# Attention values of two neighbouring groups computed in one go in the fused turns

## The chip, the cores and the metric

The kernel runs on one core of a Trainium2 chip. Its engines work side by side and meet at semaphores: TensorE (PE, with its weight loads listed apart as PEld), VectorE (DVE), ScalarE (ACT), GpSimd (POOL) and SyncE (SP), which issues DMAs. The metric is the device time of one launch in microseconds (us). The kernel before took 914.95 us (median of three runs, 913.76 to 915.36).

## The reference

One decoder layer on 16 sequences of 256 tokens with 256 channels, all in float32. Three blocks follow each other, and after each the sum with its input is normalised over the channels:

```
x = _layernorm(x + attn(x))       # 4 heads against 1024/4 fixed keys and values, relu(scores)**2, no softmax
x = _layernorm(x + xattn(x, ctx)) # 16 heads of 16 channels, softmax, below
x = _layernorm(x + ffn(x))        # 256 -> 1024 -> 256, with a low-rank addition chosen by the largest gate of 8
```

The middle block is the one that the change touches:

```
logits = jnp.einsum('bhqd,bhkd->bhqk', Q, K) * scale
D = jnp.clip(frac[:, None, :] - frac[:, :, None], CLAMP_MIN, CLAMP_MAX)
D_pos = jnp.maximum(D, 0.0)
D_neg = jnp.minimum(D, 0.0)
stoich_bias = ap * D_pos[:, None] + an * D_neg[:, None]
attn = gamma * logits + delta * stoich_bias
probs = jax.nn.softmax(attn, axis=-1)
out = jnp.einsum('bhqk,bhkd->bhqd', probs, V)
```

## The kernel before, in words

The order of the instructions on every engine is written out by hand; each engine works through its own list, and semaphores are set where one engine needs another's data or buffer.

The kernel has three stretches. In the first (to about 260 us) the eight blocks of 512 tokens go through the first attention. Then 64 groups follow, one per turn of the loop at line 1014 (index n): a group is four heads of one sequence, all 256 queries against all 256 keys. A sequence has four groups (og = n % 4): two chunks o of eight heads, and in each chunk the even heads (i = 0) and the odd heads (i = 1). A last stretch after the loop ends the feed-forward work of the last two blocks.

The stages of one group are spread over three turns. In its own turn n, PE computes the logits (L609) into four PSUM banks, on top of a bias that ACT has put there before ("positive", L600: the preload, one per bank g), DVE adds the other bias and finds the row maxima (L624), and POOL and DVE subtract them (L639). In turn n+1 PE transposes the result (L649, g = 0 to 3) and ACT takes the exponential on the way out of PSUM (L656, into `pT`). In turn n+2 `attend` (L665) multiplies it with the values and a column of ones: a *value set* of eight matmuls of a 32-column array shape, which the profile lists as 16 records, since every float32 matmul is listed twice. The set of the even heads fills one half of an accumulator bank `av`, that of the odd heads the other; after the odd one `keep` copies the bank out (L678, DVE).

From n = 15 (FIRST) to n = 62 the turns are *fused*: beside a group each turn carries an eighth of a block's feed-forward work. `tb` counts the blocks (0 to 5) and `part` (0 to 7) the eighth. Part 0 turns the block's rows (L749, copied by ACT, L752), part 1 computes the gates, parts 2 and 3 ("halved") the first large products, and parts 4 to 7 one product each with the second weights (`finish`: L860 on PE, 16 records, then L873 and statistics on DVE).

In a turn of parts 4 to 7 PE's list is: logits of group n; the value set of group n-2; transposes g = 0 and 1 of group n-1; a *large piece* (one of queries L437, project L561, keys L457, values L479, by n % 4); the product L860; transposes g = 2 and 3. ACT's list is: the exps g = 2 and 3 of the turn before, a fourth bias (L593), the preloads g = 0 and 1, exp 0, preload 2, exp 1, preload 3, and then what the part adds, in part 7 four scalings of the next block's rows (L249).

Small PSUM results go to three tiles that are handed out in rotation (`tile_b`): two of the pool psB and one of psV. A new tile may be written when the engine that read the third last one is done. The accumulator `av` has a bank of its own, `pT` two buffers.

Of the kernel before, what the change touches and what calls it, by code (L numbers as in the profile page):

```python
# [21 lines left out]
def tile_decoder_layer(ctx: ExitStack, tc: tile.TileContext, a: dict, out: bass.AP):  # L22
# [364 lines left out]
    if True:  # L387
# [296 lines left out]
        groups = [Group(batches[n // 4], n % 4) for n in range(4 * B)]  # L684
        N = len(groups)
# [209 lines left out]
    with tc.manual_schedule():  # L895
# [20 lines left out]
        for tb in range(NB):  # L916
# [24 lines left out]
            if tb > 1:  # L941
                older = rows_in[tb - 2]
# [67 lines left out]
        FUSED, FIRST = NB - 2, 15  # L1010
# [3 lines left out]
        for n in range(N + 2):  # L1014
            now, nxt, last, older = (
                groups[n + d] if 0 <= n + d < N else None for d in (0, 1, -1, -2)
            )
            large_piece, small_piece, more = pieces(n)
            tb, part = divmod(n - FIRST, 8)
            ff = rows_out[tb] if 0 <= tb < FUSED or (tb == FUSED and part < 2) else None  # L1020
            halved = ff and part in (2, 3)
# [2 lines left out]
            done = None  # L1024
            if part == 3 and 0 < tb < FUSED or (tb, part) == (FUSED, 0):
                done = rows_out[tb - 1]
            b, og = divmod(n, 4)

            if n < 2:
# [4 lines left out]
                six.gates()  # L1034
            if n > N:
                six.inner(0, range(0, 1))
            if older and not halved and n != N:
                older.attend()
            if nxt:
                nxt.negative(4 if 1 <= n < FIRST - 1 else 3)  # L1040
# [103 lines left out]
            tb, part = divmod(n - FIRST + 4, 8)  # L1144
# [116 lines left out]
```

## Time and profile before

| | |
|---|---|
| median of the runs | 914.95 us (913.76 to 915.36) |
| the profiled execution's own time | 914.93 us |
| its span | 913.1 us |
| PE busy | 892.4 us (98%) |
| DVE busy | 707.7 us (78%) |
| ACT busy | 584.2 us (64%) |
| POOL busy | 379.5 us (42%) |
| granted TensorE clock | 1.00 |
| value sets, L665 | 1024 records, 69.8 us |
| logits, L609 | 1024 records, 74.8 us |

A busy share says how long an engine had something in hand; matmuls are pipelined, so the extents of neighbouring rows overlap, and the start of one group of rows to the start of the next is the better measure of what it takes. The length of a turn is taken from its first logits to the first logits of the next turn. For the block from n = 23 to n = 30 the lengths are 7.41, 7.32, 15.34, 14.06, 9.59, 9.16, 9.16 and 9.24 us (parts 0 to 7); for the three blocks after it part 0 takes 7.14 us and parts 4 to 7 the same as here. In the last fused block, whose turns have fewer large pieces, parts 4 to 7 take 9.16, 7.43, 9.15 and 7.43 us.

### The profile page before, as it was taken

The numbers are of one execution on the slowest core, as the hardware profiler recorded it, in microseconds if no ns is written. First come the engines' busy times: TensorE is split into PE (matmuls) and PEld (weight loads), VectorE is DVE, ScalarE is ACT, GpSimd is POOL, SyncE is SP. The second block draws the span as 40 slices with busy tenths as digits, with TensorE's granted clock in tenths as the row PEclk, the third lists the DMA queues.
The fourth block names the chain that finished last, engine by engine and source line by source line (L and its number), as shares of the span: only waits on it lengthen the run. The fifth ranks groups of instructions, "written<-read, shape, count | busy, mean of one in ns | idle before, by whom it ended". The sixth has DMA issues, their size and how long they took to land.

```text
span 913.1 us, 19025 instructions
## 1 busy us (share of the span) xinstructions
PE 892.4 (98%) x6910; PEld 541.6 (59%) x6910; DVE 707.7 (78%) x1968; ACT 584.2 (64%) x977; POOL 379.5 (42%) x369
## 2 busy tenths in 40 slices
PE   6999999999999999999999999999999999999997
PEld 2333333333356776577658757865875686586555
DVE  5788899889878998778777877777787787678443
ACT  4757877787687879466666856665685567556111
POOL 1002312231469996434635543463454336244010
PEclk9999999999999999999999999999999999999999
DMA  5411011100001222010111202011120201111001
GB/s 137 146 36 35 30 36 41 65 1 2 3 11 50 70 71 56 13 42 21 35 43 39 52 13 66 18 37 41 40 52 14 65 17 40 41 27 45 23 1 47
DMA packets 44190, 37.01 MB, mean 41 GB/s; under 512 B 14912, under 2 KB 40000, under 8 KB 44096
## 3 DMA queue, kind: packets, MB, share of 16 engines
q1 hardware_dynamic: 43536, 35.52, 14.0%
q8 instruction: 55, 0.90, 0.4%
q14 instruction: 39, 0.32, 0.1%
q10 hardware_dynamic: 560, 0.26, 0.1%
HBM read 21.07 MB, written 6.03 MB: 30 GB/s over the span
## 4 chain that ended last, share of the span: by engine, by line
PE 56%; ACT 4%; DVE 1%; issue 1%; ACTq 0%; DVEq 0%
PE ps_b L860 12%; PE ps_l L830 12%; PE ps_b L649 9%; PE ps_l L609 6%; PE ps_v L665 5%; PE ps_b L561 3%; PE ps_b L457 2%; PE ps_b L479 2%; PE ps_l L842 2%; ACT ps_l L600 2%; ACT pT L656 1%; PE ps_b L437 1%; PE ps_b L749 1%; ACT qT L447 1%; DVE neg L624 1%
## 5 line engine op out<-in xcount | busy, mean ns | idle before, releaser
L588 POOL TENSOR_SCALAR neg<-dneg,aneg,delta 128x512 f32<-128x512 f32 x205 | 175.7, 869 | 211.2 <-ACT pT L656 185.8
L624 DVE CUSTOM_DVE_ANT_0 neg<-ps_l,neg 128x256 f32<-128x256 f32 x512 | 181.6, 420 | 43.0 <-PE ps_l L609 39.8
L600 ACT ACTIVATE ps_l<-dpos,apos_d 128x512 f32<-128x512 f32 x256 | 173.1, 686 | 34.5 <-DVE mx L624 30.5
L656 ACT ACTIVATE pT<-ps_b 128x512 f32<-128x512 f32 x256 | 143.3, 590 | 59.1 <-PE ps_b L649 57.4
L324 DVE TENSOR_TENSOR pr<-r 128x1024 f32<-128x1024 f32 x128 | 155.5, 1255 | 32.4 <-ACT r L322 32.1
L322 ACT ACTIVATE r<-ps_a 128x1024 f32<-128x1024 f32 x128 | 126.5, 1022 | 59.1 <-PE ps_a L314 33.9
L649 PE MATMUL ps_b<-ident,neg 128*128 128x128 f32 x1024 | 140.3, 278 | 4.0 <-ACT pT L656 2.4
L649 PEld LDWEIGHTS ps_b<-ident,neg 128*128 128x128 f32 x1024 | 112.9, 140 | 41.9 <-issue 15.3
L639 POOL TENSOR_TENSOR neg<-neg,mx 128x1024 f32<-128x1024 f32 x65 | 124.3, 1914 | 30.0 <-DVE mx L624 24.0
L314 PE MATMUL ps_a<-xnT,kT 64*64 64x512 f32 x1024 | 124.2, 601 | 0.0
L334 PE MATMUL ps_v<-pr,vv 64*64 64x512 f32 x1024 | 123.5, 593 | 0.3
L860 PE MATMUL ps_b<-wof,hT 128*128 128x256 f32 x512 | 115.8, 380 | 0.0
L830 PE MATMUL ps_l<-xt,wi 128*128 128x512 f32 x256 | 115.0, 596 | 0.8 <-ACT hT L849 0.8
L860 PEld LDWEIGHTS ps_b<-wof,hT 128*128 128x128 f32 x512 | 96.4, 190 | 16.0 <-issue 2.3
L639 DVE TENSOR_TENSOR neg<-neg,mx 128x1024 f32<-128x1024 f32 x63 | 90.9, 1443 | 0.3
L349 POOL TENSOR_TENSOR xt<-xt,half 128x512 f32<-128x512 f32 x15 | 23.7, 1583 | 141.0 <-ACT half L348 141.0
L334 PEld LDWEIGHTS ps_v<-pr,vv 64*64 64x64 f32 x1024 | 38.1, 132 | 70.7 <-issue 43.7
L314 PEld LDWEIGHTS ps_a<-xnT,kT 64*64 64x64 f32 x1024 | 38.1, 135 | 67.9 <-issue 56.2
L830 PEld LDWEIGHTS ps_l<-xt,wi 128*128 128x128 f32 x256 | 46.8, 190 | 52.0 <-issue 45.8
L609 PE MATMUL ps_l<-kM,qT 32*128 32x256 f32 x1024 | 74.8, 401 | 0.4 <-ACT ps_l L600 0.4
L665 PE MATMUL ps_v<-pT,vaug 128*32 128x256 f32 x1024 | 69.8, 385 | 0.8 <-ACT pT L656 0.8
L853 DVE TENSOR_SCALAR hT<-ps_l,wib 128x512 f32<-128x512 f32 x44 | 30.5, 745 | 42.8 <-PE ps_l L842 42.8
(107 smaller groups left out, 966.9 us busy)
## 6 DMA issues: line engine op xcount, KB each, us to landing
cT<-in_ctxT SPq DMA_DIRECT2D x16, 256.0 KB
kM<-keys SPq DMA_DIRECT2D x128, 32.0 KB
v<-raw SPq DMA_DIRECT2D x128, 32.0 KB
invs<-rows SPq DMA_DIRECT2D x128, 32.0 KB
x<-in_x SPq DMA_DIRECT2D x7, 512.0 KB
out<-x SPq DMA_DIRECT2D x7, 512.0 KB
frow<-in_frac SPq DMA_DIRECT2D x16, 128.0 KB
wi<-in_wiT SPq DMA_DIRECT2D x1, 1024.0 KB
```

What stands on the lines that cost most here:

```text
L314: nc.tensor.matmul(sc[64 * k : 64 * k + 64, h, :], lhsT=kT[64 * h : 64 * h + 64, q, hf * P + 64 * k : hf * P + 64 * k + 64], rhs=self.xnT[ ...
L324: nc.vector.tensor_tensor(pr, r, r, ALU.mult)
L334: nc.tensor.matmul(self.acc[k][64 * h : 64 * h + 64, :], lhsT=vv[64 * k : 64 * k + 64, hf, 64 * q : 64 * q + 64], rhs=pr[64 * k : 64 * k + ...
L588: nc.gpsimd.tensor_scalar(self.neg[:, g], self.batch.dneg, aneg[:, h : h + 1], delta, ALU.mult, ALU.mult,)
L600: nc.scalar.activation(banks[g], self.batch.dpos.rearrange("p j k -> p (j k)"), AF.Copy, scale=apos_d[:, h : h + 1],)
L609: nc.tensor.matmul(banks[g][:, j * S : (j + 1) * S], lhsT=self.batch.qT[rows, self.o, j * P : (j + 1) * P], rhs=self.batch.kM[rows, self.i ...
L624: nc.vector.tensor_tensor_reduce(out=self.t[:, g, j, :], in0=banks[g][:, j * S : (j + 1) * S], in1=self.neg[:, g, j, :], scale=1.0, scalar ...
L639: eng.tensor_tensor(rows, rows, top.to_broadcast([P, 4, S]), ALU.subtract)
L649: nc.tensor.transpose(ps[:, k * S + j * P : k * S + (j + 1) * P], self.t[:, g, j, k * P : (k + 1) * P], ident,)
L656: nc.scalar.activation(self.pT[:, g, :], self.ps[g], AF.Exp)
L830: nc.tensor.matmul(banks[g], lhsT=wi[:, c, f * P : (f + 1) * P], rhs=self.xT[:, c, :], start=(c == 0), stop=False,)
L860: nc.tensor.matmul(ps[:, 0:C], lhsT=self.hT[f][:, j * P : (j + 1) * P], rhs=wof[:, f, :], start=(f == 0), stop=(f == FC - 1),)
```

## The change

In the fused turns of part 5 and part 7 the value set is left out, and in the turn after each (part 6, and part 0 of the next block or, at the end, n = 63) it is computed first, straight ahead of the set that is there already. The two sets belong to the even and the odd heads of one chunk and fill the two halves of the same accumulator bank. This happens at twelve places: n = 20 + 8 tb and n = 22 + 8 tb for tb from 0 to 5. PE alone has its list changed; all operations stay, and so do the lists of the other engines.

```diff
             if part == 3 and 0 < tb < FUSED or (tb, part) == (FUSED, 0):
                 done = rows_out[tb - 1]
+
+            apart = 0 <= tb < FUSED and part in (5, 7)
             b, og = divmod(n, 4)
...
                 six.gates()
             if n > N:
                 six.inner(0, range(0, 1))
-            if older and not halved and n != N:
+            if older and not halved and not apart and n != N:
+                if 0 <= n - 1 - FIRST < 8 * FUSED and (n - 1 - FIRST) % 8 in (5, 7):
+                    groups[n - 3].attend()
                 older.attend()
             if nxt:
                 nxt.negative(4 if 1 <= n < FIRST - 1 else 3)
```

## The prediction

> **What bounds the kernel now.** I read the engine shares first, then the busy time turn by turn, then the chain that ended last, and at the end the single turns engine by engine. All times are microseconds (us) unless ns is written.
>
> ```profile
> PE 892.4 (98%) x6910; PEld 541.6 (59%) x6910; DVE 707.7 (78%) x1968; ACT 584.2 (64%) x977; POOL 379.5 (42%) x369
> ...
> 485.21:494.37 9.16, 9.16 (x74) 7.39 (x73) 7.57 (x22) 6.74 (x13) 5.28 (x5) 1.00 0.17 51
> 494.37:503.52 9.15, 9.15 (x73) 7.38 (x72) 6.79 (x25) 5.26 (x10) 4.16 (x4) 1.00 0.08 18
> 503.52:512.76 9.24, 9.24 (x74) 7.30 (x73) 8.68 (x33) 7.76 (x16) 4.69 (x4) 1.00 0.11 24
> 512.76:519.90 7.14, 7.14 (x69) 5.61 (x68) 6.14 (x22) 6.12 (x12) 4.79 (x5) 1.00 0.28 63
> ```
>
> The four rows are parts 5, 6, 7 and 0 (turns n = 28 to 31), cut at the first logits of each turn: length, then busy time of PE, PEld, DVE, ACT, POOL, granted clock, DMA. PE fills each of them at the full clock. So PE time taken out counts, but only until another engine's chain is longer than what is left. The order of work inside part 7 shows how near that is:
>
> ```profile
> 503.52 1.15 PE L609 MATMUL ps_l<-kM,qT 32*128 32x256 f32 x16
> 504.60 1.07 PE L665 MATMUL ps_v<-pT,vaug 128*32 128x256 f32 x16
> 505.60 1.09 PE L649 MATMUL ps_b<-ident,neg 128*128 128x128 f32 x8
> 506.53 1.89 PE L457 MATMUL ps_b<-cT,wk 128*128 128x256 f32 x8
> 508.26 3.70 PE L860 MATMUL ps_b<-wof,hT 128*128 128x256 f32 x16
> 511.79 1.04 PE L649 MATMUL ps_b<-ident,neg 128*128 128x128 f32 x8
> 512.76 0.50 PE L609 MATMUL ps_l<-kM,qT 32*128 32x256 f32 x4
> ...
> 506.29 1.38 ACT L600 ACTIVATE ps_l<-dpos,apos_d 128x512 f32<-128x512 f32 x2 [0.20 <-DVE mx L624]
> 507.60 0.58 ACT L656 ACTIVATE pT<-ps_b 128x512 f32<-128x512 f32 x1
> ```
>
> Columns are start, extent, engine, line, instruction. The product L860 writes the PSUM tile that held the first pair of transposes (L649), because three tiles rotate and the calls are transposes g=0, g=1, large piece (L457), product. It must wait until the first exp (L656) has read that tile: 507.60 + 0.58 = 508.18. It starts at 508.26, so **in part 7 PE already runs into that exp**. The cost is visible: from the first L457 to the late transposes are 511.79 - 506.53 = 5.26, while part 6, whose exp is early, takes 502.56 - 497.37 = 5.19 for the same work.
>
> And the exp is not held by PE. On ACT it is queued behind two preloads (L600), which wait for the first maxima (L624, DVE), which wait for the logits:
>
> ```profile
> 487.38 1.38 ACT L600 ACTIVATE ps_l<-dpos,apos_d 128x512 f32<-128x512 f32 x2 [0.27 <-DVE mx L624]
> 488.69 0.58 ACT L656 ACTIVATE pT<-ps_b 128x512 f32<-128x512 f32 x1
> ...
> 494.37 1.15 PE L609 MATMUL ps_l<-kM,qT 32*128 32x256 f32 x16
> 495.44 1.07 PE L665 MATMUL ps_v<-pT,vaug 128*32 128x256 f32 x16
> 496.44 1.09 PE L649 MATMUL ps_b<-ident,neg 128*128 128x128 f32 x8
> 497.37 1.89 PE L561 MATMUL ps_b<-wo,oT 128*128 128x256 f32 x8
> 499.10 3.62 PE L860 MATMUL ps_b<-wof,hT 128*128 128x256 f32 x16
> ```
>
> In part 5 (485.21) the exp ends at 489.27, 4.06 after the logits began; the product starts at 489.95, 4.74 after them. Slack 0.68, less some 0.08 of restart. In part 7 the exp ends 4.66 after the logits, later by 0.60 because DVE is late there (statistics and a clip from the turn before: first maxima 1.82 after the logits instead of 1.17).
>
> **The change, part by part.** No instruction is added or removed; ACT, DVE, POOL and the DMA queues keep their order. On PE 12 value sets (16 records of L665 each) leave parts 5 and 7 and stand directly ahead of the next set, in part 6 and part 0. No new wait is queued on another engine: the accumulator copy (L678) always came in the second of the two turns, after that turn's maxima (4.14 after the logits), and two sets end by about 2.94.
>
> *What the joining saves.* A set takes 496.44 - 495.44 = 1.00 from its start to the next tile shape. Its records start in four steps 0.216 apart, which is also the pitch of the product (16 records in 3.45). Four steps are 0.864; the other 0.136 is a slower first step and the change of array shape. A second set behind the first needs neither: I price it at 0.864. No two sets stand together in this trace, so the bounds are 0.864 and 1.00. I take the lower, since within one set every step after the first costs 0.216. If PE alone counted, 12 x 0.136 = 1.63 would be gained.
> The Trainium skill, page "TensorEngine Tiling (Array Packing)", section "Key Properties", says that a change of tiling mode drains the engine; this row's 0.136 agrees, and the page has no figure. The same page, under "PSUM Bottleneck", says that faster TensorE work does not speed up the emptying of PSUM, which may then be the limit. By the first rule alone the change is a gain; by the second it depends on the exp above.
>
> *Part 5 without its set, blocks 0 to 4 (n = 20, 28, 36, 44, 52).* PE reaches the product 1.00 earlier, 3.74 after the logits, but the exp still ends at 4.06. Once the exp decides, the late transposes start 511.79 - 508.18 = 3.61 after its end (from part 7): 489.27 + 3.61 = 492.88. Free running they would start at 493.40 - 1.00 = 492.40. So a wait of 0.48 is new and the part shrinks by 0.52 only, to 8.64 (n = 20: exp at 4.00, wait 0.42). The waiting product is followed on PE by the late transposes and the next logits, so all of it is on the path.
>
> *Part 7 without its set, blocks 0 to 4 (n = 22, 30, ...).* The exp decided already. Late transposes stay at 508.18 + 3.61 = 511.79, the part stays at 9.24: **the whole 1.00 is lost in waiting.** After an idle engine the restart may cost differently: after the change of shape at 458.76 the second record of a 128x256 set came 0.32 later, the same as here behind the exp, so I add nothing.
>
> *Part 6 and part 0, blocks 0 to 4.* Both grow by the second set, 0.864. In part 0 the turn transposes (L749), their copies and the last preload (L600) all follow PE, so they shift with it. In n = 23 PE waits some 0.27 at L749 for an exp that ACT delivers late (part length 7.41, others 7.14); that wait is covered now: -0.27.
>
> *Block 5.* Parts 5 and 7 (n = 60, 62) have no large piece, so the product's tile is the one of the late transposes of the turn before, free long since. n = 60/61: the full -0.14. n = 62/63: the second set needs the exps of n = 62, which ACT ends at the same time as now, behind four scalings (L249); today PE already waits 0.8 for them at L665. Gain 0.
>
> Sum: part-5 pairs 4 x (-1.00 + 0.48 + 0.864) + (-1.00 + 0.42 + 0.864) = 1.38 + 0.28 = 1.66; part-7 pairs 5 x (-1.00 + 1.00 + 0.864) - 0.27 = 4.05; block 5 -0.14. Together **+5.6**. The profiled execution took 914.93 (span 913.1 and 1.8 around it), the median of the runs is 914.95. So 914.9 + 5.6 = **920.5**, 0.6% slower. A measurement of this kernel tells about 0.2% (1.8) from no change.
>
> What the PE idles grow to matters for the clock: some 0.5 and 1.0 per turn. In this trace PE waits 0.45 at 454.21 and 8.6 once early on, and the granted clock is 9 tenths or more in all 40 slices; I price it at nothing.
> The Trainium skill, page "TensorE: Matmul & The Clock Gate", section "Why this matters for your kernels", allows gaps of about 3 us before the clock falls, which would also make it nothing.
>
> **Rivals.**
> - *PE alone decides (the other sign).* The exp comes in time and all 12 joints gain: 914.9 - 1.6 = 913.3. It needs the exp to end before about 3.5 after the logits. For it: PE is 98% busy and the chain that ended last is PE alone in these turns. Against: 4.06 and 4.66 in every one of these turns, set by logits, maxima and two preloads that the change does not touch. Chance 0.05.
> - *DVE catches up in part 7.* If the statistics and the clip were done before the logits end, the exp would come at 4.06 as in part 5 and part 7 would shrink by 0.60 more: 5 x 0.60 = 3.0, 917.5. For it: part 6 is 0.86 longer. Against: DVE's late work starts with the sum (L873) that waits for the product's end, which moves with the logits. Chance 0.06.
> - *No overlap between the two sets.* The second costs its full 1.00: 11 x 0.136 = 1.5 more (n = 63 hides it), 922.0. For it: the sets write the same accumulator bank. Against: so do the steps within one set. Chance 0.08.
> - *The wait costs more than its length*, by a fall of the clock or a later exp: above 922.5. Chance 0.03.
> - *It doesn't do what it says.* The changed kernel's PE order has 32 records of L665 in a row at twelve places, so no.
>
> **How the numbers follow.** The forecast's chance is 0.78, with its own range 919.5 to 921.5 (restart and second set each known to about 0.05 a turn, 20 turns). Range 917.2 to 922.4: it leaves out the first rival and the last. Slower by over 0.2%: forecast, second, third and fourth case, 0.95, of which I give 0.02 to errors below 916.8. Slower 0.93, same 0.02, faster 0.05.
>
> **What would show it.** Part 5 about 8.64, part 6 10.02, part 7 9.24 as before, part 0 8.00. A PE wait at L860 released by ACT pT (L656), about 0.5 in part 5 and 1.0 in part 7; 32 records of L665 in about 1.94 instead of 2 x 1.07. First maxima still 1.17 and 1.82 after the logits. It would be wrong if the first exp ended earlier than 4.06 after the logits, or if part 6 or part 0 grew by less than 0.8.

## The result

The changed kernel takes 919.79 us (median of six runs, 919.4 to 920.09) against 914.37 us for the kernel before, measured beside it (six runs, 913.76 to 915.36). The ratio is 1.0058, with a 95% interval from 1.0045 to 1.0071: slower by 5.4 us, where 5.6 were forecast.

The profiled execution of the changed kernel took 919.97 us, its span is 918.2. Its engine shares (first part of the page), and then the busy time of the turns n = 28 to 31 (parts 5, 6, 7 and 0; length, busy time of PE, PEld, DVE, ACT, POOL, granted clock, DMA):

```profile
PE 891.6 (97%) x6910; PEld 542.2 (59%) x6910; DVE 707.6 (77%) x1968; ACT 584.6 (64%) x977; POOL 379.2 (41%) x369
...
485.55:494.19 8.64, 8.42 (x57) 6.88 (x56) 7.54 (x22) 6.74 (x13) 5.27 (x5) 1.00 0.18 54
494.19:504.21 10.02, 10.02 (x89) 7.90 (x89) 6.80 (x25) 5.35 (x10) 4.16 (x4) 1.00 0.08 20
504.21:513.44 9.23, 8.42 (x57) 6.88 (x56) 8.67 (x33) 7.76 (x16) 4.70 (x4) 1.00 0.09 20
513.44:521.45 8.01, 8.01 (x86) 6.16 (x85) 6.15 (x22) 6.21 (x12) 4.79 (x5) 1.00 0.26 63
```

Parts 6 and 0 grew by some 0.87 each in these rows and are still full of PE work. Part 5 lost 0.52 of the 1.00 that was taken out of it, and part 7 lost nothing: it has 8.42 of PE work and lasts 9.23, as long as before. The granted clock is 1.00 in all four. What PE waits for is listed by the waits of PE (what waited and for whom: total, times, longest); four lines of the list:

```profile
PE ps_b L860 <- ACT pT L656: 5.1, 10, 0.8
PE ps_b L649 <- ACT pT L656: 2.4, 6, 0.5
PE ps_b L649 <- ACT qT L447: 1.4, 6, 0.2
PE ps_v L665 <- ACT pT L656: 0.8, 1, 0.8
```

The first of these is new; the other three stood in the profile before with the same totals, and the lines left out, all with one wait each, changed by 0.7 at most. Ten waits of the product for an exp are the five parts 5 and the five parts 7 of blocks 0 to 4. In part 7 (n = 30, the timeline: start, extent, engine, line, instruction) the wait is this one:

```profile
504.21 1.15 PE L609 MATMUL ps_l<-kM,qT 32*128 32x256 f32 x16
505.29 1.09 PE L649 MATMUL ps_b<-ident,neg 128*128 128x128 f32 x8
506.22 1.89 PE L457 MATMUL ps_b<-cT,wk 128*128 128x256 f32 x8
508.92 3.72 PE L860 MATMUL ps_b<-wof,hT 128*128 128x256 f32 x16 [0.81 <-ACT pT L656]
512.48 1.04 PE L649 MATMUL ps_b<-ident,neg 128*128 128x128 f32 x8
...
506.97 1.38 ACT L600 ACTIVATE ps_l<-dpos,apos_d 128x512 f32<-128x512 f32 x2 [0.20 <-DVE mx L624]
508.29 0.58 ACT L656 ACTIVATE pT<-ps_b 128x512 f32<-128x512 f32 x1
```

In part 5 (n = 28, logits at 485.55) it is the same wait, but shorter, since the exp ends earlier, at 489.62, 4.06 after the logits before rounding:

```profile
489.67 3.72 PE L860 MATMUL ps_b<-wof,hT 128*128 128x256 f32 x16 [0.22 <-ACT pT L656]
...
489.04 0.58 ACT L656 ACTIVATE pT<-ps_b 128x512 f32<-128x512 f32 x1
```

In part 7 the exp ends at 508.87, 4.66 after the logits as before, and the product starts 0.05 later. The exp's result, `pT`, is no operand of the product, which reads `wof` and `hT`; so it is the tile that the exp reads which the product waits for. Read forward, the chain of work that ended last says the same. In the kernel before it is PE alone here (start, length, what; n = 29 to 30):

```profile
499.27 3.45 PE ps_b L860 x16
502.72 0.87 PE ps_b L649 x8
503.59 1.07 PE ps_l L609 x16
504.67 1.00 PE ps_v L665 x16
505.67 1.02 PE ps_b L649 x8
506.69 1.73 PE ps_b L457 x8
508.42 3.53 PE ps_b L860 x16
```

In the changed kernel it leaves PE at the end of part 6, goes through DVE's statistics, clip and first maxima, ACT's two preloads and the exp, and comes back to PE at the product of part 7:

```profile
499.95 3.47 PE ps_b L860 x16
...
503.44 0.43 DVE x L873
...
504.54 0.57 DVE dneg L494
...
506.16 0.26 DVE neg L624
...
506.97 1.38 ACT ps_l L600 x2
508.35 0.52 ACT pT L656
508.88 0.04 issue
508.92 3.72 PE ps_b L860 x16
```

Turn by turn (first logits to first logits), this is where the time went; the columns on the right are the experiments below:

| turns | part | before | changed | part 5 alone | part 7 alone | exp first | before, exp first | clip later |
|---|---|---|---|---|---|---|---|---|
| 20 | 5 | 9.16 | 8.58 | 8.58 | 9.16 | 8.15 | 9.16 | 8.58 |
| 28, 36, 44, 52 | 5 | 9.16 | 8.64 | 8.64 | 9.16 | 8.15 | 9.16 | 8.64 |
| 21 to 53 | 6 | 9.16 | 10.02 | 10.02 | 9.16 | 10.02 | 9.16 | 10.02 |
| 22 to 54 | 7 | 9.24 | 9.24 | 9.24 | 9.24 | 8.15 | 9.15 | 8.63 to 8.65 |
| 23 | 0 | 7.41 | 8.01 | 7.41 | 8.00 | 8.01 | 7.41 | 8.01 |
| 31, 39, 47, 55 | 0 | 7.14 | 8.00 | 7.14 | 8.01 | 8.01 | 7.14 | 8.00 |
| 60 / 61 | 5 / 6 | 7.43 / 9.15 | 6.43 / 10.02 | 6.43 / 10.02 | 7.43 / 9.16 | 6.43 / 10.02 | 7.43 / 9.16 | 6.43 / 10.02 |
| 62 | 7 | 7.43 | 6.43 | 7.43 | 6.43 | 6.43 | 7.43 | 6.43 |
| n = 0 to 62, all | | 569.70 | 574.25 | 571.36 | 572.90 | 566.73 | 569.43 | 571.26 |
| n = 63 to the end | | 83.72 | 84.72 | 83.72 | 84.72 | 84.59 | 84.25 | 84.73 |

The turns that share a row agree within 0.02 us (but in the run with the exp first, n = 55 takes 8.08). Turns that are not listed agree between the kernels within 0.03, but for n = 9 and n = 12, which differ by up to 0.05; all of them together are 0.13 to 0.15 longer in the four columns from "part 5 alone" to "before, exp first" than in the kernel before, almost all of it ahead of the fused turns. The last stretch, from the logits of n = 63 on, took 1.00 longer in the changed kernel, so the turns account for 4.55 + 1.00 = 5.55. The stretch ahead of n = 0 varied from 258.8 to 260.1 between these executions, though no kernel touches it; this is why single spans differ by less (918.2 - 913.1 = 5.1).

### The profile page after: what moved, and what is told of

The parts are those of the page before. It is cut to its first block, busy times and chain, and to the rows that moved or that the text cites. A ratio compares the mean times of both kernels' runs of the same rounds, so it can differ in the third digit from the quotient of the medians.

```text
span 918.2 us, 19025 instructions
## 1 busy us (share of the span) xinstructions
PE 891.6 (97%) x6910; PEld 542.2 (59%) x6910; DVE 707.6 (77%) x1968; ACT 584.6 (64%) x977; POOL 379.2 (41%) x369
## 4 chain that ended last, share of the span: by engine, by line
PE 50%; ACT 8%; DVE 3%; issue 1%; ACTq 0%; DVEq 0%
PE ps_b L860 12%; PE ps_l L830 12%; PE ps_b L649 7%; PE ps_v L665 5%; PE ps_l L609 4%; ACT ps_l L600 3%; PE ps_b L561 3%; ACT pT L656 2%; PE ps_b L479 2%; PE ps_l L842 2%; PE ps_b L457 1%; DVE neg L624 1%; ACT xt L752 1%; DVE st L189 1%; ACT qT L447 1%
## 5 line engine op out<-in xcount | busy, mean ns | idle before, releaser
L624 DVE CUSTOM_DVE_ANT_0 neg<-ps_l,neg 128x256 f32<-128x256 f32 x512 | 181.6, 420 | 41.4 <-PE ps_l L609 39.1
L656 ACT ACTIVATE pT<-ps_b 128x512 f32<-128x512 f32 x256 | 143.6, 591 | 60.3 <-PE ps_b L649 57.8
L860 PE MATMUL ps_b<-wof,hT 128*128 128x256 f32 x512 | 116.4, 382 | 5.1 <-ACT pT L656 5.1
L860 PEld LDWEIGHTS ps_b<-wof,hT 128*128 128x128 f32 x512 | 96.0, 190 | 23.8 <-ACT pT L656 9.1
L665 PE MATMUL ps_v<-pT,vaug 128*32 128x256 f32 x1024 | 67.5, 384 | 0.8 <-ACT pT L656 0.8
```

The costliest lines, as they stand in the source:

```text
L624: nc.vector.tensor_tensor_reduce(out=self.t[:, g, j, :], in0=banks[g][:, j * S : (j + 1) * S], in1=self.neg[:, g, j, :], scale=1.0, scalar ...
L656: nc.scalar.activation(self.pT[:, g, :], self.ps[g], AF.Exp)
L860: nc.tensor.matmul(ps[:, 0:C], lhsT=self.hT[f][:, j * P : (j + 1) * P], rhs=wof[:, f, :], start=(f == 0), stop=(f == FC - 1),)
```

## The experiments

The theory: the joint itself gains 0.136 us; what costs is that parts 5 and 7, without the set, run into the first exp, which waits on ACT behind the preloads and the maxima. The rivals: the joined sets cost time in themselves; PE's waiting has another cause (DVE as the bound of part 7, or the *roots* on ACT, two short instructions, L198 and L200, which stand ahead of the preloads in part 7 and wait for DVE's statistics).

**One pair at a time.** First part 5 alone, then part 7 alone:

```diff
-            apart = 0 <= tb < FUSED and part in (5, 7)
+            apart = 0 <= tb < FUSED and part == 5
...
-                if 0 <= n - 1 - FIRST < 8 * FUSED and (n - 1 - FIRST) % 8 in (5, 7):
+                if 0 <= n - 1 - FIRST < 8 * FUSED and (n - 1 - FIRST) % 8 == 5:
```

> Only the sets of part 5 are joined to those of part 6; parts 7 and 0 as before. Theory (the product L860 waits for the first exp): part 5 8.64 us (n = 20: 8.6), part 6 10.02, part 7 9.24, part 0 7.14; in all 0.28 + 4 x 0.34 - 0.13 = +1.5 us on 914.4, so about 915.9. Rival (the joined sets themselves cost time, each of the twelve the same): half of the +5.4, 917.1. Rival (PE alone): 913.6.

Measured: 916.55 us against 914.78 (ratio 1.0020, 1.0011 to 1.0028), +1.8.

The second kernel has 7 in the place of 5.

> Only the sets of part 7 are joined to those of part 0. Theory: part 7 stays 9.24 us, part 0 grows from 7.14 to 8.00; in all 5 x 0.86 - 0.27 = +4.0 us on 914.4, so about 918.4. Rival (each of the twelve costs the same): 917.1. Rival (PE alone): 913.6.

Measured: 918.56 us against 914.78 (ratio 1.0042, 1.0029 to 1.0055), +3.8. The two halves do not cost the same: the intervals, +1.0 to +2.6 and +2.7 to +5.0, exclude each other, and the two add up to 5.6, about the 5.4 of the change. By the turns the first is 571.36 - 569.70 = +1.66, of which 1.53 lie in parts 5 and 6 (worked out: 1.52); the second is 572.90 - 569.70 = +3.20 and another 1.00 from n = 63 on, +4.2, of which 4.05 lie in part 0 (worked out: 4.05). The rest, 0.13 and 0.15, lies in turns without any joint. PE's waits at L860 for the exp are five in either kernel, 1.0 in all in the first and 4.1 in the second. That joined sets cost the same wherever they stand is excluded.

**The exp ahead of the preloads.** The set stays out of parts 5 and 7, and PE's list is that of the changed kernel. Only ACT takes the first exp earlier:

```diff
+                if apart:
+                    last.turned(0)
+                    last.exps(0)
                 if nxt:
                     nxt.positive(0)
                     nxt.positive(1)
-                if last:
+                if last and not apart:
                     last.turned(0)
                     last.exps(0)
```

> As the changed kernel, but in parts 5 and 7 ACT takes the first exp ahead of the first two preloads, so that it no longer waits for the maxima. PE's list is the same as in the changed kernel. Theory: the first exp ends about 2.4 us after the logits, the product no longer waits, part 5 and part 7 shrink to about 8.16 us, parts 6 and 0 stay at 10.02 and 8.00; eleven joints gain 0.136 each and part 7 loses its old wait of 0.08, in all 914.4 - 1.5 - 0.4 = about 912.5. Rival (the joined sets, or PE's idle time, cost the time in some other way): near 919.8 still. Rival (DVE, 8.7 us busy in part 7, becomes the bound there): part 7 about 8.7, 915.

Measured: 912.53 us against 914.78 (ratio 0.9976, 0.9966 to 0.9986): faster than the kernel before by 2.2, and than the changed kernel by 7.3 between the medians, 7.7 by the turns and the last stretch. The same four turns (n = 28 to 31) of this kernel, then part 7 on its timeline:

```profile
485.08:493.24 8.16, 8.16 (x58) 6.97 (x57) 7.22 (x22) 6.61 (x13) 5.28 (x5) 1.00 0.19 58
493.24:503.26 10.02, 10.02 (x90) 7.91 (x89) 7.05 (x25) 5.35 (x10) 4.17 (x4) 1.00 0.09 20
503.26:511.41 8.15, 8.15 (x57) 6.96 (x57) 7.94 (x32) 7.30 (x16) 4.70 (x4) 1.00 0.07 15
511.41:519.42 8.01, 8.01 (x86) 6.16 (x85) 6.70 (x23) 6.37 (x13) 4.77 (x5) 1.00 0.25 61
```

```profile
505.26 1.89 PE L457 MATMUL ps_b<-cT,wk 128*128 128x256 f32 x8
506.99 3.62 PE L860 MATMUL ps_b<-wof,hT 128*128 128x256 f32 x16
...
505.28 0.30 ACT L198 ACTIVATE ln<-mv,epst 128x4 f32<-128x4 f32 x1 [0.66 <-DVE mv L190]
505.61 0.20 ACT L200 ACTIVATE near<-ln 128x4 f32<-128x4 f32 x1
505.72 0.58 ACT L656 ACTIVATE pT<-ps_b 128x512 f32<-128x512 f32 x1
506.20 1.90 ACT L600 ACTIVATE ps_l<-dpos,apos_d 128x512 f32<-128x512 f32 x3
```

The exp now ends at 506.30, 3.04 after the logits, ahead of the product's 3.73, and PE fills all four turns. (About 2.4 was expected; that came in part 5, 2.43, while in part 7 the exp stands behind the two roots.) Its waits for L656 at L860 are gone from the list. Parts 6 and 0 with their two sets are as long as in the changed kernel (but for n = 55), so joining the sets does not cost time in itself, and DVE, with 7.94 of 8.15 us busy, does not bind part 7 at this length.

**The early exp without the joints.** The same edit on the kernel before, in parts 5 and 7:

> The kernel before with the first exp ahead of the preloads in parts 5 and 7, no sets joined. Theory: only the old wait of 0.08 us in part 7 goes, five times, 914.4 - 0.4 = 914.0; so what the run before this one gains comes from the joints. Rival (an early exp gains by itself): 912.5 as there.

Measured: 915.06 us against 914.78 (ratio 1.0004, 0.9995 to 1.0013), no difference that can be told. Part 7 did become 9.15 instead of 9.24 in each of the five blocks, 0.4 in all, which is less than the runs resolve. The rest of the time shows what the expectation left out: the last stretch is 0.53 longer (84.25 against 83.72). In n = 62 ACT now idles until PE has come past the set to the transposes that the first exp reads, and everything behind it on ACT is late. The scalings (L249) start 827.19 - 820.99 = 6.20 after the logits instead of 827.66 - 822.00 = 5.66, and in n = 63 the value set, which needs the exps behind them, stretches from 1.29 to 1.82. First the kernel before, then this one:

```profile
822.00 1.15 PE L609 MATMUL ps_l<-kM,qT 32*128 32x256 f32 x16
827.66 2.07 ACT L249 ACTIVATE x<-hid,nm,rs 128x256 f32<-128x256 f32 x4
830.51 1.29 PE L665 MATMUL ps_v<-pT,vaug 128*32 128x256 f32 x16
```

```profile
820.99 1.15 PE L609 MATMUL ps_l<-kM,qT 32*128 32x256 f32 x16
823.76 0.60 ACT L656 ACTIVATE pT<-ps_b 128x512 f32<-128x512 f32 x1 [0.81 <-PE ps_b L649]
827.19 2.07 ACT L249 ACTIVATE x<-hid,nm,rs 128x256 f32<-128x256 f32 x4
829.50 1.82 PE L665 MATMUL ps_v<-pT,vaug 128*32 128x256 f32 x16
```

An early exp is therefore worth next to nothing while the set still stands in front of it, and the joint less than nothing without it; the gain of 2.2 needs both.

**Why part 7 is worse than part 5.** In part 7 the first maxima start late because DVE still has statistics and a clip from the turn before. In this kernel, otherwise the changed one, the clip is done a turn later, at the end of part 7 (and likewise of part 3 instead of part 2):

```diff
             if og == 1:
-                return older and older.project(), None, [later and (lambda: later.clip("dneg"))]
+                return older and older.project(), None, []
             if og == 2:
-                return nxt and nxt.keys(), None, [later and (lambda: later.clip("dpos"))]
+                return nxt and nxt.keys(), None, [
+                    later and (lambda: later.clip("dneg")), later and (lambda: later.clip("dpos"))
+                ]
```

> As the changed kernel, but the clip of the next fractions that DVE does at the end of parts 2 and 6 (L494, dneg, 0.66 us) is done at the end of parts 3 and 7, together with the other one. Theory (the first exp of part 7 is late because DVE reaches the maxima late): first maxima of part 7 about 0.58 earlier, 1.24 us after the logits instead of 1.82, first exp ending at 4.08 instead of 4.66, part 7 of blocks 0 to 4 8.65 us instead of 9.24; part 0 keeps 8.00, as PE has two sets there. In all 5 x 0.58 = 2.9 less than the changed kernel. Rival (part 7 is held by something else, the roots on ACT or the joined sets): part 7 stays 9.24.

Measured, in a single run on another chip: 917.35 us, and 913.96 for the kernel before beside it. One run can not carry a difference of three microseconds, but the turns can: part 7 takes 8.63 to 8.65 in blocks 0 to 4, 0.60 less than in the changed kernel, all other turns agree within 0.04, and the turns together take 571.26 against 574.25, 3.0 less. Part 7 (n = 30, logits at 504.01) on its timeline, DVE and then ACT:

```profile
505.35 0.42 DVE L624 CUSTOM_DVE_ANT_0 neg<-ps_l,neg 128x256 f32<-128x256 f32 x1
...
506.17 1.38 ACT L600 ACTIVATE ps_l<-dpos,apos_d 128x512 f32<-128x512 f32 x2 [0.20 <-DVE mx L624]
507.48 0.58 ACT L656 ACTIVATE pT<-ps_b 128x512 f32<-128x512 f32 x1
```

The first maxima start 1.34 after the logits, where they start 1.95 after them in the changed kernel (506.16 in the chain above), and the exp ends at 4.05 instead of 4.66. So the 0.61 by which DVE was late in part 7 reached PE in full. What is left of PE's wait there is that of part 5: the ten waits at the product are 2.1 in all, none longer than 0.2. The roots are not what holds the preloads: in n = 30 of the changed kernel the second one ends 0.20 before the preloads start, and it is the maxima that release them (the mark [0.20 <-DVE mx L624] above). (The prediction counted the maxima from the event 0.13 ahead of the first row, in part 5 and in part 7 alike: 1.82 and 1.17.)

## Why the prediction was right

*What the joining saves.* 32 records of L665 take 497.13 - 495.27 = 1.86 in part 6 where two sets apart took 2.00: 0.14 for each joint, 0.86 for the second set. The lower of the two bounds was the right one, and the rival without overlap (922.0) falls.

The sets on the timeline of the changed kernel, part 6 of n = 29:

```profile
495.27 1.93 PE L665 MATMUL ps_v<-pT,vaug 128*32 128x256 f32 x32
497.13 1.09 PE L649 MATMUL ps_b<-ident,neg 128*128 128x128 f32 x8
```

*Part 5 without its set.* Worked out 8.64 and, for n = 20, 8.58; measured 8.64 and 8.58. The exp ended at 4.06 (4.00) as before, since neither the maxima nor the preloads depend on the set.

*Part 7 without its set.* Worked out 9.24, measured 9.23 to 9.24. The rival that DVE would catch up in part 7 (917.5) did not come by itself: DVE's late work starts when the product of part 6 ends and moves with the logits (the chain above). The run with the clip later shows that its price was right: 3.0 were named, and 3.0 came when the lateness was removed by hand.

*Parts 6 and 0.* Worked out +0.86 each, measured +0.86 and +0.86; n = 23 grew by 0.60 where 0.59 had been worked out, as its old wait was covered.

*Block 5.* n = 60/61 gained 0.13 (0.14 worked out). n = 62 became 1.00 shorter, and the transposes after the sets of n = 63 came 3.29 after its logits instead of 2.29 (836.75 - 833.46; 831.73 - 829.43, 2.29 before rounding): all of it was given back, as the second set still waits for the exps of n = 62 behind the four scalings. The term of 0 holds, but one reading behind it does not: the wait of 0.8 at L665 that the prediction places here stands at n = 15 (351.94 in the trace). In n = 63 of the kernel before, the set took 831.73 - 830.51 = 1.22 instead of 1.00, so PE lost 0.22 there. That the exps decide is right, and with PE 1.00 earlier they decide all the more.

*The sum.* 5.6 against 5.5 in the turns and 5.4 in the medians. The rival that PE alone decides, 913.3, is about what the changed kernel would have been with the exp out of its way: the run with the exp first is at 912.5, which is close to that less the 0.4 and 0.3 of the old waits in part 7 and n = 23.

One sign was announced at the wrong size, though the lengths were right. The prediction expected to see PE waits of about 0.5 in part 5 and 1.0 in part 7; the profile shows 0.22 and 0.81, and 5.1 in all, though by the lengths of the turns ten waits cost 0.42 + 4 x 0.48 + 5 x 1.08 = 7.7. The record ahead of the wait has an extent of 0.38 where the pitch is 0.216, and the idle time is only counted from its end; and the second record behind the wait comes after 0.32 instead of 0.216. The two make up the missing 0.27 of each wait. The lengths from start to start are the measure, as they were for the forecast. (The prediction read this 0.32 behind the exp of the kernel before, too; there it is 0.30. It added nothing for the restart, and the 3.61 from the exp's end to the late transposes came out in all ten turns.)

## What to carry to other kernels

A stretch in which one engine is 98% busy can still stand at the edge of another engine's chain: before work is moved out of it, look up when the buffer that the next step needs is released, and compare that time, counted from the start of the stretch, with the time the engine would get there. Here 0.14 us per joint was to be had and up to 1.00 per joint was lost to a PSUM tile whose reader stood behind two preloads that could come later in these turns. Moving that reader ahead in its own engine's list turned the loss of 5.4 us into a gain of 2.2. Made alone, it gained 0.4 in part 7 and lost 0.5 in n = 63, since its engine then idled for the reader's input: a reader is to be moved ahead only as far as its input is ready.

## What the runs showed of the hardware

A restart of PE at the product cost about 0.10 us, the second record coming 0.32 after the first instead of 0.216, and it cost no more after 0.81 us of idle time than after 0.22. From the exp's end to the late transposes it was 3.61 in part 5 and part 7 alike (512.48 - 508.87 in n = 30), and 3.61 in part 7 of the kernel before, where PE had hardly stopped. The granted clock stayed at 1.00 in these turns. Not expected, and not explained here: the stretch ahead of the first group took 258.8 to 260.1 us in seven executions of kernels that share it instruction for instruction, while single turns repeat within 0.02; a change of a microsecond in this kernel is read from the turns and not from one span.
